# Four moves in the last quarter of a two-layer graph kernel: prefix sum, statistics, a second DMA queue, a view per indirect store

## The chip, the cores and the metric

The kernel runs on one core of one Trainium2 chip. The metric is device time of an execution in microseconds (us), median of several executions. The kernel before takes 683.77 us (median of 3 runs, 682.87 to 683.98). A profile is one such execution; its span is about 1.7 us shorter than the time.

## The reference

Two layers on N = 2708 nodes with D = 512 features, followed each by a layer norm (cut):

```python
def _L0_gnn_ref(x, adj, W, b):
    d_inv_sqrt = jnp.where(rowsum > 0, rowsum ** (-0.5), 0.0)
    support = (d_inv_sqrt[:, None] * adj * d_inv_sqrt[None, :]) @ x
    return jax.nn.relu(support @ W + b)
def _L1_gnn_ref(nodes, adj, W_node, b_node, K, ...):      # attention, 4 heads
    ...
    logits = s[:, :, None] + NEG * (1.0 - adj)[None]      # NEG = -1e10
    attn = jax.nn.softmax(logits, axis=-1)
    ...                                                   # mean over heads, relu
x = _layernorm(x + _L0_gnn_ref(...)); x = _layernorm(x + _L1_gnn_ref(...))
```

The entries of `adj` lie between 0.05 and 1, so NEG * (1 - adj) leaves each row of the second layer a single neighbour, that of its largest entry. The kernel therefore gathers one row of u = relu(h·M + c) per node (M and c fold the weights together) and checks on the chip that this held; a dense path stands ready if not.

## The kernel before

The first layer runs over eleven pairs of row blocks (m = 0 to 10), each in eleven steps of k (at_k = 0 to 10). A step turns four adjacency tiles on TensorE, ScalarE copies them to SBUF, VectorE makes four sums of them, and TensorE multiplies. After a pair, VectorE combines the products, and the rows of the pair before go through h·M. A block is 128 rows (74 in the last pair, blocks 20 and 21). The program's order on each engine is the order of the source.

While the last pair runs, the gathers for blocks 0 to 15 go out, eight ahead of the statistics. Rows whose neighbour lies in the last pair must wait for its u, so they are set aside in a list: a flag marks them, a prefix sum of the flags (two small matmuls) gives each its place, and GpSimd turns the places into one-hot rows, with which TensorE writes the list. These "listed rows" are gathered and written last, by two indirect stores.

The parts that the change touches, and those that the argument needs:

```python
def store(dst, t, ib):
    for lo, hi, r0 in parts(ib):          # two parts for a block of 74 rows
        nc.sync.dma_start(out=dst[r0 + lo : r0 + hi, :], in_=t[lo:hi])
...
out_early, out_late = dram_disjoint_views(out, 2)
...
def ahead(i):                             # transposes and copies for step i
    ...
    nc.scalar.copy(aT[:kr, :4, :pr], ps[:kr, :, :pr])
    nc.vector.tensor_add(s(S1), s(L21), s(L22))   # and three more
...
def store_u(ib, po):
    nc.vector.tensor_add(ut[:pr], po[:pr], c_bc[:pr])
    nc.scalar.activation(ut[:pr], ut[:pr], AF.Relu)
    store(u_late if ib >= NE else u_early, ut, ib)        # NE = 20
...
def fetch_row(ib):                        # an indirect DMA from GpSimd
    gs[ib] = mix.tile([P, D], F32, name="g", bufs=8)
    fetch(gs[ib], pr, idx[:pr, ib : ib + 1], u_d if ib >= NE else u_early)
...
for i, (m, k) in enumerate(steps):
    ...
    if m == NM - 3 and at_k == NM - 1:    # NM = 11
        ps = counts(flag_b)               # prefix sum: two matmuls
    ahead(i + 2)
    ...
    products(i, banks, at_k == 0, at_k == NM - 1)
    ...
    elif final:                           # the last pair
        if at_k == 0:
            home(0); home(1)              # ten loads of 256 KB, own rows
        elif at_k == 2:
            for ib in range(*chunk(0)):   # blocks 0 to 4
                fetch_row(ib)
        elif at_k == 3:
            for ib in range(PER, PER + 3):
                fetch_row(ib)             # blocks 5 to 7
            for n in range(NL):           # NL = 2 blocks of listed rows
                fetch(hs[NB + n], P, to_read[:, n : n + 1], h_d)
        elif 6 <= at_k:
            n = (at_k - 6) * 2
            for ib in (n, n + 1):
                stats(ib, P)              # add, bn_stats, bn_aggr on VectorE
                if n + 8 < 16:
                    fetch_row(ib + 8)
            if at_k == 8:   home(2); home(3); spread(*chunk(0))
            elif at_k == 9: shift_of(*chunk(0)); chunk_out(0)
            elif at_k == 10: spread(*chunk(1))
    if at_k == NM - 1:
        new = combine(m, banks)           # opens with nc.scalar.copy(s1, p1)
...                                       # tail: last two blocks, chunks 1 to 3
for n in range(NL):                       # rows whose neighbour lies in the last pair
    normalize(NB + n, P)
    nc.gpsimd.indirect_dma_start(out=out_early[:, :], ...)
```

`chunk_out(c)` normalizes five blocks on ScalarE and stores each through SyncE's queue.

## Time and profile before

| | kernel before |
|---|---|
| time, median of 3 | 683.77 us |
| the profiled execution | 689.2 us, span 687.4 us |
| TensorE stands for the prefix sum at | 519.8 to 523.0 us, half clock after it |
| TensorE's last product of the last pair ends | 629.21 us |
| first addition of the last combination | 637.35 us |
| second indirect store issued | 682.57 us |

The page's line of busy times gives each engine's busy us, its share of the span and its instructions:

```profile
PE 621.2 (90%) x2810; PEld 460.1 (67%) x2810; DVE 471.6 (69%) x1166; ACT 170.8 (25%) x245; POOL 96.9 (14%) x135
```

TensorE (PE) carries the kernel up to about 630 us, so the averages of the others say little: what matters is who keeps TensorE or the tail waiting, and where. Note the first two rows of the table: the execution that was profiled took 5.4 us more than the timed ones. That turns out to matter.

### The profile page before, as it was taken

To read this page: it belongs to the slowest core of one execution; us is meant where nothing else is said; L and a number is where in the kernel's file an instruction comes from. 1 tells how busy PE (TensorE), PEld (TensorE's weight loads), DVE (VectorE), ACT (ScalarE), POOL (GpSimd) and SP (SyncE) were. 2 spreads that over 40 slices of the span, in tenths; PEclk is the share of its full clock that TensorE was granted. 3 is DMA by queue.
4 is the path that set the end of the run, shared out by engine and by line. 5 is a ranking of instruction groups with operands and counts; after the bars stand their busy time and mean duration, and the time that the engine had idled before them with its cause. 6 is when DMAs were issued, how large, how long until landed. Compare 5 with 4: busy or idle time off the path is not lost. (4 is left out here: it accounts for less than half of the span.)

```text
span 687.4 us, 7915 instructions
## 1 busy us (share of the span) xinstructions
PE 621.2 (90%) x2810; PEld 460.1 (67%) x2810; DVE 471.6 (69%) x1166; ACT 170.8 (25%) x245; POOL 96.9 (14%) x135
## 2 busy tenths in 40 slices
PE   5999979999999999999999999999998999996420
PEld 3545434787878878878788788787886787563100
DVE  2356886998785856957858569578587479329773
ACT  2544455111112121211121212111211111201333
POOL 1011321000000001000000010000002260055442
PEclk9999999999999999999999999999997999998565
DMA  8999899213050141410501414104014010758743
GB/s 340 417 379 403 329 366 301 92 33 161 31 193 31 60 187 39 172 53 31 193 31 59 188 39 173 51 32 192 31 60 97 31 62 0 251 163 272 238 137 118
DMA packets 30774, 103.73 MB, mean 151 GB/s; under 512 B 4169, under 2 KB 4169, under 8 KB 25568
## 3 DMA queue, kind: packets, MB, share of 16 engines
q1 hardware_dynamic: 28008, 96.30, 38.2%
q0 software_dynamic: 2720, 6.86, 3.3%
q8 instruction: 24, 0.39, 0.2%
q14 instruction: 22, 0.18, 0.1%
HBM read 85.64 MB, written 17.77 MB: 150 GB/s over the span
## 5 line engine op out<-in xcount | busy, mean ns | idle before, releaser
L360 PE MATMUL bank<-v,aT 128*128 128x256 f32 (+3 forms) x968 | 270.1, 382 | 0.4 <-DVE t L382 0.4
L360 PE MATMUL bank<-t,aT 128*128 128x256 f32 (+3 forms) x726 | 197.9, 381 | 1.2 <-DVE u L387 0.8
L360 PEld LDWEIGHTS bank<-v,aT 128*128 128x128 f32 (+3 forms) x968 | 171.8, 187 | 23.5 <-DVE t L382 0.6
L360 PEld LDWEIGHTS bank<-t,aT 128*128 128x128 f32 (+3 forms) x726 | 135.7, 187 | 24.0 <-DVE u L387 1.2
L333 ACT COPY aT<-tp 128x512 f32<-128x512 f32 (+3 forms) x121 | 68.5, 568 | 263.6 <-PE tp L331 246.4
L338 DVE TENSOR_TENSOR aT<-aT 128x128 f32<-128x128 f32 (+3 forms) x121 | 33.9, 281 | 88.4 <-ACT aT L333 87.4
L197 PE MATMUL po<-w_sb,sT 128*128 128x512 f32 (+1 forms) x176 | 79.9, 598 | 3.3 <-DVE sT L191 3.3
L197 PE MATMUL po<-m_sb,sT 128*128 128x512 f32 (+1 forms) x176 | 81.1, 615 | 0.0
L331 PE MATMUL tp<-ident,a 128*128 128x128 f32 (+3 forms) x484 | 71.3, 270 | 0.3 <-ACT aT L333 0.3
L421 DVE MAX8 top<-a 128x8 f32<-128x1354 f32 (+1 forms) x44 | 68.8, 1563 | 0.0
L422 DVE FIND_INDEX8 at<-top,a 128x8 uint32<-128x1354 f32 (+1 forms) x44 | 68.7, 1562 | 0.0
L331 PEld LDWEIGHTS tp<-ident,a 128*128 128x128 f32 (+3 forms) x484 | 58.2, 139 | 14.6 <-issue 5.3
L272 ACT ACTIVATE junk<-a 128x2708 bf16<-128x2708 f32 (+1 forms) x22 | 54.1, 2461 | 47.9 <-DMA a<-in_adj_dram 47.9
L408 POOL TENSOR_SCALAR rs<-mv 128x1 f32<-128x1 f32 (+1 forms) x22 | 7.7, 350 | 398.5 <-DVE mv L406 398.5
L197 PEld LDWEIGHTS po<-m_sb,sT 128*128 128x128 f32 (+1 forms) x176 | 33.9, 194 | 40.7 <-issue 40.1
L197 PEld LDWEIGHTS po<-w_sb,sT 128*128 128x128 f32 (+1 forms) x176 | 31.4, 188 | 36.9 <-issue 32.9
L430 DVE TENSOR_TENSOR ut<-po,c_bc 128x512 f32<-128x512 f32 (+1 forms) x22 | 15.1, 690 | 41.2 <-PE po L197 41.2
L270 DVE COPY v<-po 128x512 f32<-128x512 f32 (+1 forms) x22 | 15.2, 690 | 34.3 <-PE po L197 34.3
L431 ACT ACTIVATE ut<-ut 128x512 f32<-128x512 f32 (+1 forms) x22 | 13.8, 630 | 100.2 <-DVE ut L430 96.5
L341 DVE TENSOR_TENSOR aT<-aT 128x128 f32<-128x128 f32 (+3 forms) x121 | 35.1, 290 | 4.2
L340 DVE TENSOR_TENSOR aT<-aT 128x128 f32<-128x128 f32 (+3 forms) x121 | 33.7, 279 | 0.0
L339 DVE TENSOR_TENSOR aT<-aT 128x128 f32<-128x128 f32 (+3 forms) x121 | 33.7, 279 | 0.0
(137 smaller groups left out, 433.3 us busy)
## 6 DMA issues: line engine op xcount, KB each, us to landing
a<-in_adj_dram SPq DMA_DIRECT2D x38, 1354.0 KB
v<-in_x_dram SPq DMA_DIRECT2D x20, 256.0 KB
xr<-in_x_dram SPq DMA_DIRECT2D x20, 256.0 KB
h_d<-t SPq DMA_DIRECT2D x20, 256.0 KB
u_d<-ut SPq DMA_DIRECT2D x20, 256.0 KB
a<-h_d SPq DMA_DIRECT2D x20, 256.0 KB
out_dram<-a SPq DMA_DIRECT2D x20, 256.0 KB
kh<-in_L_gnn_K_dram SPq DMA_DIRECT2D x3, 1024.0 KB
```

Of the source, the lines that this page charges most:

```text
L197: nc.tensor.matmul(po[:pr], sT[:, f, :pr], wt[:, f, :], start=(f == 0), stop=(f == ND - 1))
L270: nc.vector.tensor_copy(v[:pr, ib, :], po[:pr])
L272: nc.scalar.activation(junk[:pr], a[:pr], AF.Copy, accum_out=sums[:pr, ib : ib + 1])
L331: nc.tensor.transpose(ps[:kr, q, :pr], raw[m][q // 2][:pr, lo : lo + kr], ident[:pr, :pr])
L333: nc.scalar.copy(aT[:kr, :4, :pr], ps[:kr, :, :pr])
L338: nc.vector.tensor_add(s(S1), s(L21), s(L22))
L339: nc.vector.tensor_sub(s(S3), s(L11), s(L21))
L340: nc.vector.tensor_sub(s(S2), s(S1), s(L11))
L341: nc.vector.tensor_sub(s(S4), s(L12), s(S2))
L360: nc.tensor.matmul(banks[bank][:pr, side, :], aT[:kr, left, :pr], right, start=first and side == 0, stop=last, skip_group_check=True,)
L421: nc.vector.max(out=top[:pr, ib, hf, :], in_=part)
L422: nc.vector.max_index(out=at[:pr, ib, hf, :], in_max=top[:pr, ib, hf, :], in_values=part)
```

## The change

Four things, each meant to take a wait off the path: the prefix sum's matmuls move behind other work of TensorE (with the ranks and one-hot rows that hang on them); the statistics of the gathered blocks move from steps 6 to 10 of the last pair to steps 5 to 9; u of the last four blocks is stored from ScalarE's DMA queue, not behind the loads in SyncE's; and each indirect store gets its own view of the output, so that the second needn't wait for the first.

```diff
-    def store(dst, t, ib):
+    def store(dst, t, ib, queue=nc.sync):
...
-            nc.sync.dma_start(out=dst[r0 + lo : r0 + hi, :], in_=t[lo:hi])
+            queue.dma_start(out=dst[r0 + lo : r0 + hi, :], in_=t[lo:hi])
-    out_early, out_late = dram_disjoint_views(out, 2)
+    out_views = dram_disjoint_views(out, 1 + NL)
+    out_late = out_views[NL]
...
-        store(u_late if ib >= NE else u_early, ut, ib)
+        store(u_late if ib >= NE else u_early, ut, ib, nc.scalar if ib >= NE - 2 else nc.sync)
...
-            store(out_early, hs[ib], ib)
+            store(out, hs[ib], ib)
...
-        if m == NM - 3 and at_k == NM - 1:
+        if m == NM - 2 and at_k == 0:
             ps = counts(flag_b)
...   (ranks, one-hot rows and listing: one step later each)
-            elif 6 <= at_k:
-                n = (at_k - 6) * 2
-                for ib in (n, n + 1):
+            if 5 <= at_k < 10:
+                for ib in range(at_k * 2 - 10, at_k * 2 - 8):
                     stats(ib, P)
-                    if n + 8 < 16:
+                    if ib + 8 < 16:
                         fetch_row(ib + 8)
...   (spread and shift_of: a step sooner; chunk_out and home stay in steps 9 and 8)
-            out=out_early[:, :],
+            out=out_views[n][:, :],
```

More of the change, by code (lines that the diff above doesn't have):

```diff
@@ L627, in tile_two_graph_layers @@
             hTs[2 * (m - 1) + q] = turn(done[q], rows(2 * m - 2), nc.scalar.copy)
-        if m == NM - 3:
-            if at_k == NM - 2:
-                flag, flag_b = first_indices()
-            elif at_k == NM - 1:
+        if m == NM - 3 and at_k == NM - 2:
+            flag, flag_b = first_indices()
+        if m == NM - 2:
+            if at_k == 0:
                 rank = ranks(flag, ps)
-        elif m == NM - 2:
-            if at_k < 5:
-                for ib in range(at_k * 4, at_k * 4 + 4):
+            if 1 <= at_k < 6:
+                for ib in range(at_k * 4 - 4, at_k * 4):
                     hot(rank, ib)
-            if at_k == 2:
+            if at_k == 3:
                 ls = p_o.tile([P, D], F32, name="po")
-            if 2 <= at_k < 7:
-                for ib in range(at_k * 4 - 8, at_k * 4 - 4):
+            if 3 <= at_k < 8:
+                for ib in range(at_k * 4 - 12, at_k * 4 - 8):
                     enlist(ls, ib)
@@ L666, in tile_two_graph_layers @@
                 nc.vector.tensor_copy(bad_i, po[:1, :1])
-            elif 6 <= at_k:
-                n = (at_k - 6) * 2
-                for ib in (n, n + 1):
+            if 5 <= at_k < 10:
+                for ib in range(at_k * 2 - 10, at_k * 2 - 8):
                     stats(ib, P)
-                    if n + 8 < 16:
+                    if ib + 8 < 16:
                         fetch_row(ib + 8)
-                if at_k == 8:
-                    home(2)
-                    home(3)
-                    spread(*chunk(0))
-                elif at_k == 9:
-                    shift_of(*chunk(0))
-                    chunk_out(0)
-                elif at_k == 10:
-                    spread(*chunk(1))
+            if at_k == 7:
+                spread(*chunk(0))
+            elif at_k == 8:
+                home(2)
+                home(3)
+                shift_of(*chunk(0))
+            elif at_k == 9:
+                chunk_out(0)
+                spread(*chunk(1))
         if at_k == NM - 1:
```

## The prediction

> **What bounds the kernel now.** I read the page first. Its busy rows show TensorE full from about slice 7 to slice 36, and one dent in the row of the granted clock.
>
> ```profile
> span 687.4 us, 7915 instructions
> ...
> PE   5999979999999999999999999999998999996420
> ...
> PEclk9999999999999999999999999999997999998565
> ```
>
> One digit is 17.2 us. The dent (a 7) is at 515 to 533 us; after 629 us TensorE is nearly done and the end belongs to others. So a microsecond counts in two places: where TensorE stops before 629 us, and on the path after it. Next I asked who kept TensorE waiting after 500 us (the waits of PE: the waiter, whom it waited for, total us, times, longest).
>
> ```profile
> PE tp L189 <- DVE t L415: 16.9, 2, 16.3
> PE po L475 <- DVE flag_b L470: 3.3, 1, 3.3
> PE tp L189 <- ACT aT L333: 0.3, 1, 0.3
> ```
>
> The second line is the prefix sum's matmul, the first the gap of the last pair. The timeline of PE there (start, duration):
>
> ```profile
> 519.17 0.59 PE L360 MATMUL bank<-v,aT 128*128 128x256 f32 x2
> 523.02 0.17 PE L475 MATMUL po<-flag_b,before 128*128 128x20 bf16 x1 [3.25 <-DVE flag_b L470]
> ...
> 525.66 1.91 PE L360 MATMUL bank<-t,aT 74*128 74x256 f32 x4
> ...
> 529.93 8.36 PE L197 MATMUL po<-m_sb,sT 128*128 128x512 f32 x16
> 538.13 0.60 PE L331 MATMUL tp<-ident,a 128*128 128x128 f32 x4
> ```
>
> TensorE stands still for 3.25 us, and afterwards four products take 1.91 us where they took 1.03 before. The stage view from 523 to 532 us gives a granted clock of 0.50, and 1.00 on either side. For the last pair I read the timelines of ACT, DVE and POOL:
>
> ```profile
> 610.38 0.41 ACT L333 COPY aT<-tp 128x296 f32<-128x296 f32 x1 [3.14 <-PE bank L360]
> 618.37 0.71 ACT L333 COPY aT<-tp 128x296 f32<-128x296 f32 x2 [7.58 <-PE tp L331]
> ...
> 633.43 3.63 ACT L579 ACTIVATE a<-a,nbs,rss 128x512 f32<-128x512 f32 x5 [12.81 <-DVE nbs L575]
> 636.97 0.35 ACT L381 COPY s<-bank 74x256 f32<-74x256 f32 x1
> ```
>
> ```profile
> 603.87 1.26 POOL L553 DMA_INDIRECT g<-u_d,idx  x1 [17.65 <-DMA u_d<-ut]
> ...
> 678.94 1.05 POOL L744 DMA_INDIRECT out_dram<-listed,to_put  x1 [1.84 <-ACT listed L579]
> 682.57 0.99 POOL L744 DMA_INDIRECT out_dram<-listed,to_put  x1 [2.58 <-issue]
> ```
>
> TensorE's last product ends at 629.2 us, but the copy that opens its combination (L381) starts at 636.97 and the first add (L382) at 637.35: 8 us late. VectorE is still in the statistics (to 636.3) and ScalarE in five normalizations queued ahead of the copy. From there one chain runs to the end: combine, layer norm, turn, times M, u, its store, the gathers from 661.94, statistics, normalization, two indirect stores. The second store waits 2.58 us.
>
> **What the Trainium skill says.** "TensorE: Matmul & The Clock Gate", Part 1, states that an idle window of about 3.4 us halves the clock and that the window is free-running. The trace agrees: 3.25 us idle, then 0.50. "DMA: Bandwidth & Descriptors", section "Issuing engines are not separate DMA queues", says that DMAs from different engines run on the same 16 engines and interleave; its section "Queues, rings and completion order" gives SP and ACT each a ring and lets an engine go round-robin between them. No transfer of this trace was issued by ACT, so it can't show that yet. The section "Anatomy of one DMA" of the same page gives a fixed cost of some 2 us to completion; the second store's wait of 2.58 us agrees.
>
> **The change, part by part.**
>
> 1. Prefix sum a step on. The step view of PE (start to start of its transposes) is 3.46 us for a plain step and 10.33 us for a pair's last step with its two products by M, in each of the seven pairs before. Here the two are 6.93 and 15.06 (523.07 to 538.13): 8.20 us too long, of which 3.3 is the wait and the rest half clock. In the new order the matmul stands behind the eight products by M (about 7 us of work), so flag_b, ready at 522.96, is long there. That removes 8.2 us; two small matmuls cost about 0.15. What it moves: the ranks (13 VectorE operations, 525.84 to 528.0, 2.15 us) leave the path to the combination and go into a step where VectorE idles. The 20 one-hot rows on GpSimd begin later. Before, four were made at 528.24 to 531.9, far ahead; now each group has two steps (7.4 us) less two small operations of the layer norm. Four take 3.7 to 3.9 us against a step of 3.70, and the layer norm's pair of POOL operations (0.9 us) comes in twice. By my count the rows 8 to 11 are ready 0.75 us after TensorE wants them and the rest nearly on time: TensorE loses about 0.8. Net 8.2 - 0.15 - 0.8 = **7.2 us**, all on the path, since the last pair follows TensorE.
>
> 2. Statistics a step sooner. A block costs 0.68 + 0.69 + 0.18 us, 1.53 from start to start; a step of two blocks and the aT adds (0.85) is about 4.0 us against TensorE's 3.28. Started after the adds that end at 611.6 (the gathers landed 3 to 4 us after issue, so blocks 0 and 1 are there), five such rounds, the last without adds, end at about 629.9. The five normalizations run 626.8 to 630.5, the copy follows, the combination starts at about 630.9 instead of 637.35: 6.5 us in this profile. But here the first block began only at 619.53, because the copy ready to start at 613.6 was held until 618.37 by something the trace does not explain (TensorE's transposes had ended). Without that hold the old order would have begun at 614.9 and combined at 633.2: a gain of only 2.3 us. The profiled run took 689.2 us and the timed ones 683.8, so part of this hold may not be there in the timed runs. I chose **3.8 us**, nearer the low end.
>
> 3. u stored from ScalarE's queue. Before, the stores were issued at 596.20 and 598.36 behind ten loads of 256 KB on SP's ring, and the first gather went at 603.87. On its own ring I estimate 2 us sooner. With part 2 the statistics begin at 611.6, after even the old gathers had landed (607.6 and on), so this is hidden. At the end SP's ring is empty when u goes out (654.7 to 659.6); a hop between engines, **0.2 us**. ScalarE pays 0.3 to 0.5 us per issue, where it has room.
>
> 4. A view per indirect store. In the built program the second store no longer waits for the first. POOL's gathers start 1.25 us apart, so it goes at 680.2 instead of 682.57: 2.4 us sooner, less some sharing as both move 256 KB together: **2.2 us**, at the very end.
>
> Sum: 7.2 + 3.8 + 0.2 + 2.2 = 13.4 us; 683.8 - 13.4 = **670.4 us**.
>
> **The rivals.**
>
> - The hold of ScalarE's copy is real, and either goes (then the statistics bring 6.5: 667.7 us) or moves with the gathers, 2 us earlier, onto the copy of the step before. Then the statistics start only at about 616 and the gain falls to 1.5 us: 672.7. For it: the hold ends as the gathers end. Against it: nothing in the dependencies ties them.
> - GpSimd becomes the bound in the one-hot stretch: 20 rows of 0.95 us in five steps of 3.7. If TensorE waits 2 to 3 us there, and especially if the clock halves again, half of part 1 goes back: about 674 to 676 us. Against it: a wait of under 1 us by my count, in pieces.
> - The end is bound by moving bytes, so two indirect stores together land no sooner: 672.6. Against it: 256 KB landed within 2.4 us of the end of issue, most of it fixed.
> - The clock at the last products by M falls differently. In the profile eight logical products took 9.39 us there against 7.03 at full clock; this is worth up to 1.2 us either way.
>
> **Range and chances.** The parts vary from 10.5 us (statistics 1.5, one-hots 1.5 worse) to 16.5 (hold real and gone), hence 667.0 to 674.0 us for 8 in 10. 2% of 683.8 is 13.7 us, so the line is at 670.1, just below my number: faster by over 2% 0.45, within 2% 0.54, slower 0.01. Every part removes a wait that the trace shows on the path or is hidden, so slower is remote.
>
> **What would show it.** Right: no wait of PE for flag_b and no half clock before the last pair; steps of 3.46 and about 10.5 us there; PE's last product at about 622 us; the first add of the combination within 2 us of it; the second indirect store 1.3 us after the first; the first gather within 4 us of the second u store. Wrong: PE waits for a hot row above 1 us in total; ScalarE's copies of the last pair held again, with VectorE idle before the statistics; the second store landing late.

## The result, and the profile after

The changed kernel took 673.55 us (median of 4, 673.23 to 675.08), the kernel before 683.32 us in the same call (median of 4). All were in the fast state. The ratio is 0.9861, 95% interval 0.9843 to 0.988: within 2%. (A ratio is the mean time of one kernel's fast runs over that of the other's in the same rounds, so not quite the ratio of the medians.) That is 9.8 us gained where 13.4 were predicted; the time lies inside the range.

The page of the kernel after, the lines that answer to those shown of before:

```profile
span 671.5 us, 7913 instructions
...
PE   5999988999999999999999999999999999999420
...
PEclk9999998999999999999999999999999999999675
```

The dent in the clock at three quarters of the span is gone. From the waits of TensorE in the kernel after, 500 to 690 us (columns as in the prediction), the one that is new:

```profile
PE po L513 <- POOL hot L508: 0.6, 1, 0.6
```

Its timeline of TensorE where the prefix sum now stands:

```profile
520.33 0.60 PE L332 MATMUL tp<-ident,a 128*128 128x128 f32 x4
523.79 7.03 PE L198 MATMUL po<-m_sb,sT 128*128 128x512 f32 x16
530.65 0.17 PE L476 MATMUL po<-flag_b,before 128*128 128x20 bf16 x1
530.71 0.64 PE L332 MATMUL tp<-ident,a 128*128 128x128 f32 x4
```

The step is 3.46 us and the next 10.38, as in other pairs; the prefix sum follows the products by M without a gap, and those take 7.03 us where they took 8.36 at half clock. The only wait for a one-hot row is 0.6 us. ScalarE's timeline in the last pair of the kernel after:

```profile
610.41 0.41 ACT L334 COPY aT<-tp 128x296 f32<-128x296 f32 x1 [2.88 <-DVE mvs L567]
613.70 0.40 ACT L334 COPY aT<-tp 74x296 f32<-74x296 f32 x1 [2.88 <-PE tp L332]
619.94 3.63 ACT L580 ACTIVATE a<-a,nbs,rss 128x512 f32<-128x512 f32 x5 [5.84 <-DVE nbs L576]
623.48 0.35 ACT L382 COPY s<-bank 74x256 f32<-74x256 f32 x1
```

And GpSimd's timeline, the first gather and the two indirect stores:

```profile
597.69 1.26 POOL L554 DMA_INDIRECT g<-u_d,idx  x1 [17.98 <-issue]
...
665.00 1.05 POOL L743 DMA_INDIRECT out_dram<-listed,to_put  x1 [1.84 <-ACT listed L580]
666.35 0.99 POOL L743 DMA_INDIRECT out_dram<-listed,to_put  x1 [0.30 <-issue]
```

No copy of ScalarE is held here: they come every 3.3 us. The normalizations start at 619.94 and the first addition comes at 623.86, 1.2 us after TensorE's last product. The second indirect store waits 0.30 us instead of 2.58.

To compare traces whose starts differ by a microsecond, I measure the last pair from one mark: the set of four transposes just ahead of the eight products by M of the pair before (574.68 us before, 568.16 after). The expectations below call it the pair's first transposes; it is in fact the second set, but the same in every run. From the mark to the first addition it was 62.67 us before and is 55.70 after. That is 7 us, not the 3.8 that I gave the statistics. With the prefix sum's 7.25 us (from a common point at 516.14 and 516.87 us to the mark, 58.54 and 51.29 us) and 2.4 us of the tail, the two profiles differ by nearly 16 us. The timed runs differ by 9.8. So the profile of before probably shows something that its timed runs had not: the hold of ScalarE's copy. (This is inferred: no trace of the kernel before from a call in which it took 683 us was kept.) Of the 2.4 us of the tail, 1.1 go with the clock of TensorE's last products by M, which took 9.39 us before and 8.27 after; over all fourteen profiles they lie anywhere from 8.23 to 9.73 us.

### The profile page after: what moved, and what is told of

It is laid out like the page before. It is cut to its first block, busy times and chain, and to the rows that moved or that the text cites. A ratio compares the mean times of both kernels' runs of the same rounds, so it can differ in the third digit from the quotient of the medians.

```text
span 671.5 us, 7913 instructions
## 1 busy us (share of the span) xinstructions
PE 616.4 (92%) x2810; PEld 457.8 (68%) x2810; DVE 472.4 (70%) x1166; ACT 171.0 (25%) x245; POOL 98.8 (15%) x135
## 4 chain that ended last, share of the span: by engine, by line
PE 73%; DVE 16%; POOL 4%; DMA 2%; issue 2%; ACT 1%; POOLq 0%; SPq 0%; ACTq 0%; DVEq 0%
PE bank L361 44%; PE po L198 20%; PE tp L332 6%; PE tp L190 3%; DVE at L423 2%; DVE top L422 2%; POOL hot L508 2%; DMA g<-u_d,idx 1%; DVE st L566 1%; DVE km L279 1%; DMA v<-in_x_dram 1%; DVE a L564 1%; PE po L303 1%; DVE v L217 1%; DVE aT L342 1%
## 5 line engine op out<-in xcount | busy, mean ns | idle before, releaser
L198 PE MATMUL po<-m_sb,sT 128*128 128x512 f32 (+1 forms) x176 | 78.6, 600 | 0.0
```

What stands on the lines that cost most here:

```text
L198: nc.tensor.matmul(po[:pr], sT[:, f, :pr], wt[:, f, :], start=(f == 0), stop=(f == ND - 1))
```

## The experiments

All runs were correct and in the fast state. The kernel before ran beside each, but not at the same speed in every call: 683.3 us in the call above, 688.91 in that of the first four runs below, 688.88 and 688.17 in the next two, and 683.44 in the last. I therefore compare ratios, and traces of like calls.

Distances from the mark, in us, from each run's trace. The copies of the last pair usually start 3.3 us apart; one that starts over 4 us after the one before it is called held:

| run | parts of the change | TensorE's last product | first addition | held copies |
|---|---|---|---|---|
| before, first profile | none | 54.53 | 62.67 | yes |
| before_again | none | 54.54 | 62.42 | yes |
| prefix_only | prefix | 54.53 | 62.29 | yes |
| stats_only | statistics | 58.71 | 61.85 | yes |
| views_only | views | 55.29 | 62.00 | yes |
| queue_only | queue | 54.53 | 61.67 | yes |
| after, first profile | all | 54.53 | 55.70 | no |
| after_again | all | 60.62 | 62.26 | yes |
| no_stats | all but statistics | 56.09 | 62.65 | yes |
| no_queue | all but queue | 56.53 | 61.51 | yes |
| early_queue | queue only half | 57.98 | 61.98 | yes |
| copies_dve | no queue, copies moved | 59.95 | 62.29 | yes |
| thin_gathers | no queue, fewer gathers ahead | 54.53 | 55.47 | no |
| thin_late_stats | the same, statistics late | 54.53 | 59.02 | no |

### before_again: is the hold a matter of one profile?

The kernel before, unchanged.

> The kernel before, unchanged, profiled a second time. Theory 1: the hold of ScalarE's aT copy (610.8 to 618.4 us in the first profile) was an event of that one profiled run; then no copy of the last pair waits over 3.3 us, the first add of the last combination comes about 4 us sooner after the pair's start than the 52.5 us of the first profile (so about 48), and the span is about 682. Theory 2: the hold belongs to the order of the program; then it is there again, over 6 us, with a span near 687. Timed: a ratio of 1.000 within 0.2% in either case.

It took 689.03 us, ratio 1.000 (0.9991 to 1.0009). In its trace the same copy is held: it should follow the one at 611.30 by 3.3 us and starts at 619.02. In this call the timed runs, too, take 689. So the hold is no accident of one profile; the theory that it was fell. It belongs to a call (that is, perhaps, to a chip), and the first profile of before was of that kind while its timed runs were not.

### prefix_only, stats_only, views_only, queue_only: each part alone

Each applies the hunks of one part of the diff above to the kernel before, and nothing else:

```diff
 # prefix_only
-        if m == NM - 3 and at_k == NM - 1:
+        if m == NM - 2 and at_k == 0:
             ps = counts(flag_b)
...   (ranks, one-hot rows and listing a step later)
 # stats_only
-            elif 6 <= at_k:
+            if 5 <= at_k < 10:
...
 # views_only
-            out=out_early[:, :],
+            out=out_views[n][:, :],
 # queue_only
-        store(u_late if ib >= NE else u_early, ut, ib)
+        store(u_late if ib >= NE else u_early, ut, ib, nc.scalar if ib >= NE - 2 else nc.sync)
```

> Only the prefix sum a step on. From the profile: the wait for flag_b and the half clock before the last pair are gone (8.2 us), one-hot rows cost about 0.8, so 7.3 us faster, about 676.0, ratio 0.9893. Rival: part of it is given back in the last pair, because TensorE runs ahead of the gathers and statistics; then 4 to 6 us.

> Only the statistics a step sooner. Theory 1 (no hold in a usual run): the combination starts at most 2.3 us sooner, so 0 to 2.3 us, ratio 0.9966 to 1.000. Theory 2 (hold in every run, cured by the new order): 5 to 6.5 us, ratio 0.990 to 0.993. If the gathers were the bound (first gather at 603.9): the statistics wait for them and the gain is near 0.

> Only the view per indirect store. The second store goes 1.3 us after the first instead of 3.6: 2.2 us faster, ratio 0.9968. Rival: both stores share the DMA engines and land no sooner: 0 to 0.8 us.

> Only u stored from ScalarE's queue. Hidden: ratio 1.000 within 0.1%, hold in the trace as before. Rival: it cures the hold, 3 to 5 us faster where before takes 689.

| run | time, us | before in the same call | ratio (95%) |
|---|---|---|---|
| prefix_only | 680.97 | 688.91 | 0.9884 (0.9866 to 0.9902) |
| stats_only | 688.75 | 688.91 | 0.9993 (0.9983 to 1.0002) |
| views_only | 687.31 | 688.91 | 0.9977 (0.9963 to 0.999) |
| queue_only | 690.64 | 688.88 | 1.0021 (1.0012 to 1.0031) |

The prefix sum brings 8.0 us, the views 1.6. The statistics bring nothing that the interval shows, and the queue costs 1.5 us. ScalarE's timeline in stats_only tells why the first of these failed:

```profile
618.76 0.41 ACT L333 COPY aT<-tp 128x296 f32<-128x296 f32 x1 [6.37 <-PE tp L331]
625.90 0.70 ACT L333 COPY aT<-tp 128x296 f32<-128x296 f32 x2 [6.73 <-remote]
634.21 3.63 ACT L579 ACTIVATE a<-a,nbs,rss 128x512 f32<-128x512 f32 x5 [7.61 <-DVE nbs L575]
```

Now two copies are held, by about 3.5 and 3.8 us, instead of one by 4.4. The statistics stand behind those copies in VectorE's order, so they start 7 us sooner (613.1 us against 620.2 in before_again), but the normalizations that close them start at 634.21 against 634.08. TensorE's last product, which waits for the second held copy, slips from 630.1 to 635.0. All that was won at the start of the statistics is lost inside them. That the new order moved the hold isn't shown, though: views_only, with the old order, also has two held copies (by 2.0 and 2.5 us), so the place of the hold differs between single profiles. In GpSimd's timeline of views_only the second indirect store waits as little as in the changed kernel:

```profile
678.44 1.05 POOL L745 DMA_INDIRECT out_dram<-listed,to_put  x1 [1.84 <-ACT listed L580]
679.80 0.99 POOL L745 DMA_INDIRECT out_dram<-listed,to_put  x1 [0.30 <-issue]
```

### after_again, no_stats, no_queue: the change whole, and less one part

```diff
 # no_stats, against the changed kernel
-            if 5 <= at_k < 10:
+            elif 6 <= at_k:
...
 # no_queue, against the changed kernel
-        store(u_late if ib >= NE else u_early, ut, ib, nc.scalar if ib >= NE - 2 else nc.sync)
+        store(u_late if ib >= NE else u_early, ut, ib)
```

> The changed kernel, unchanged, a second time. Four profiles of the old order of the gathers show ScalarE's copy of the last pair held for 4 to 5 us while gathers run; the one profile of the changed kernel does not, but it came from another call, in which the kernel before took 683.3 and not 688.9 us. If the hold belongs to the call (its chip), then in a call where before takes about 689 this kernel shows it too and the ratio stays near 0.986. If the change cures it, then such a call gives about 673.5, ratio 0.977.

> The changed kernel with the statistics a step later, as before (parts 1, 3 and 4). If the statistics are worth nothing, as in their run alone (0.9993), this is as fast as the changed kernel: 0.1% either way. If they are worth the 3.8 us of the prediction once TensorE runs ahead: 0.55% slower than the changed kernel.

> The changed kernel with u stored from SP's queue (parts 1, 2 and 4). The first gather came 29.5 us after the start of the last pair's first transposes with ScalarE's queue and 28.9 to 29.2 with SP's, so no earlier: the same time as the changed kernel within 0.1%. Rival: the hold of ScalarE's copy comes with SP's queue and goes with ScalarE's; then 2 to 5 us slower, with the hold in the trace.

Beside a kernel before of 688.88 us, after_again took 680.0 (ratio 0.9862, 0.9829 to 0.9894), no_stats 680.25 (0.9869, 0.9837 to 0.99), and no_queue 678.52 (0.9844, 0.9813 to 0.9875). So the change wins about 9 us here as well, but from a start 5.5 us higher, and its trace now has the hold. The same kernel with and without the hold can be set side by side: its first addition comes at 62.26 and 55.70 us from the mark, 6.6 us apart, and its timed runs, 680.0 and 673.55 us, are 6.5 us apart. Leaving out the statistics costs 0.25 us: again they bring nothing that the intervals show. Leaving out the queue gains 1.5 us by the medians, as much as it cost alone; the ratios' intervals overlap, but the four runs of no_queue (678.06 to 678.77) all lie below the four of after_again (678.79 to 680.5). By its median no_queue is better than both kernels of the case in this call.

ScalarE's timeline in after_again:

```profile
602.57 0.41 ACT L334 COPY aT<-tp 128x296 f32<-128x296 f32 x1 [3.15 <-PE tp L332]
610.48 0.41 ACT L334 COPY aT<-tp 128x296 f32<-128x296 f32 x1 [7.50 <-PE tp L332]
616.95 0.71 ACT L334 COPY aT<-tp 128x296 f32<-128x296 f32 x2 [6.06 <-PE tp L332]
```

TensorE's timeline in the same run:

```profile
613.98 0.23 PE L332 MATMUL tp<-ident,a 74*74 74x74 f32 x1 [1.72 <-issue]
615.38 0.22 PE L332 MATMUL tp<-ident,a 74*74 74x74 f32 x1 [1.17 <-issue]
```

The copy that should start at 605.9 starts at 610.48, and TensorE lets single transposes through, 1.2 to 1.7 us apart, with no wait that the profile can name. The transposes that ScalarE's held copy names as releaser had ended at 605.8. GpSimd's gathers, meanwhile, go out every 1.25 us. A rival would be that the engines wait for their own instructions, which have DMA queues of their own in the profile. The DMA view speaks against it, though no run tests it: from 602 to 617 us it lists the gathers' queue alone, and the next packet of an instruction queue comes at 617.5 to 618, after the second held copy had started (616.95).

The queue's cost shows in the tail. ScalarE's timeline there in after_again (ACTq is the issue of DMAs from ScalarE):

```profile
646.66 1.30 ACTq L101 DMA_DIRECT2D u_d<-ut  x2
649.89 0.63 ACT L432 ACTIVATE ut<-ut 74x512 f32<-74x512 f32 x1 [3.25 <-DVE ut L431]
650.54 1.02 ACTq L101 DMA_DIRECT2D u_d<-ut  x2
651.61 3.63 ACT L580 ACTIVATE a<-a,nbs,rss 128x512 f32<-128x512 f32 x5 [1.09 <-DVE a L564]
```

And in no_queue:

```profile
649.48 0.63 ACT L432 ACTIVATE ut<-ut 74x512 f32<-74x512 f32 x1 [3.25 <-DVE ut L431]
650.38 3.63 ACT L580 ACTIVATE a<-a,nbs,rss 128x512 f32<-128x512 f32 x5 [0.27 <-DVE nbs L576]
```

Two stores of 1.02 us together stand before the five normalizations, which start 1.09 us after ScalarE's last work rather than 0.27. Their stores to the output then start later (652.45 us against 651.25), and the last gathers are late too: from the issue of the first of these (653.89 and 653.49 us) to VectorE's first use of it it takes 9.1 us with the queue and 7.7 without. And the queue brought the first gather no sooner: it is issued 29.5 us after the mark in the changed kernel, 29.2 before, 29.0 in queue_only and 28.9 in prefix_only. In the kernel before, the first u store did stand 1.3 us behind the loads (u ready at 594.90 us, store at 596.20), but the second, for which the gathers wait too, did not (598.33 and 598.36): it is issued 23.68 us after the mark before and 23.63 after. From there to the first gather it took 5.5 us before and 5.9 after.

### early_queue: is the queue's cost all in the tail?

```diff
-        store(u_late if ib >= NE else u_early, ut, ib)
+        store(u_late if ib >= NE else u_early, ut, ib, nc.scalar if NE - 2 <= ib < NE else nc.sync)
```

> The change without its new queue, plus that queue for the u of the next to last pair alone (blocks 18 and 19), not for the last two blocks in the tail. Theory A (the queue costs only in the tail: there ScalarE issues four stores of 0.5 to 0.65 us each between the two activations and the normalizations of the third chunk, so that chunk's stores start 1.2 us later and run into the last gathers): the cost goes, the ratio to the kernel before is that of the version without the queue, 0.984, and the third chunk's first normalization comes no more than 0.4 us after its shift. Theory B (the landing of u through the second queue costs too): about 0.986, and the first gather comes later than 28.9 us after the last pair's first transposes.

It took 679.41 us beside 688.17 (ratio 0.9867, 0.9842 to 0.9891). The third chunk's first normalization comes at most 0.27 us after its shift, as theory A has it, and from the last activation of u to the second indirect store it is 22.0 us (23.8 in after_again, 22.3 in no_queue), so the tail's cost is gone in the profile. But the ratio is not that of no_queue; the first gather was issued 29.7 us after the mark, and the intervals overlap. This is inconclusive: part of the queue's cost may lie before the tail.

### copies_dve: is it ScalarE that is held?

Without the queue, and with the copies of steps 6 to 10 of the last pair on VectorE:

```diff
-        nc.scalar.copy(aT[:kr, :4, :pr], ps[:kr, :, :pr])
+        if m == NM - 1 and k >= 6:
+            nc.vector.tensor_copy(aT[:kr, :4, :pr], ps[:kr, :, :pr])
+        else:
+            nc.scalar.copy(aT[:kr, :4, :pr], ps[:kr, :, :pr])
```

> The change without its new queue, with the copies of the transposed tiles for the last pair's steps 6 to 10 on VectorE. Theory S1 (ScalarE alone is held, and VectorE and TensorE wait behind it): the hold goes, the statistics of ten blocks take 18 to 20 us as in the profile of the changed kernel without the hold, rather than 24.5, and the ratio is about 0.977 to 0.979. Theory S2 (what holds ScalarE holds whatever engine copies there, or TensorE's transposes are late themselves): the copies on VectorE are late by as much, statistics again in 24 us, ratio 0.984 or above.

679.72 us beside 688.17, ratio 0.9869 (0.9843 to 0.9894). VectorE's timeline has the copies late in the same places:

```profile
610.43 0.47 DVE L335 COPY aT<-tp 128x296 f32<-128x296 f32 x1 [2.41 <-PE tp L332]
...
617.57 0.47 DVE L335 COPY aT<-tp 128x296 f32<-128x296 f32 x1 [2.76 <-remote]
```

Their starts are 6.8 and 7.1 us after the copy before, where 3.3 is usual. Theory S1 falls: whatever holds ScalarE's copy holds VectorE's too. The releaser named is again a set of transposes that had ended at 606.9 us.

### thin_gathers: do the gathers bring on the hold?

Without the queue. Four buffers for gathered blocks 0 to 15, so that a gather waits for the statistics of the fourth block before it; four others for blocks 16 to 19; and the two gathers of listed rows in the pair's last step:

```diff
-        gs[ib] = mix.tile([P, D], F32, name="g", bufs=8)
+        late = 16 <= ib < NE
+        gs[ib] = mix.tile([P, D], F32, name="g2" if late else "g", bufs=4)
...
-                for ib in range(*chunk(0)):
+                for ib in range(4):
                     fetch_row(ib)
...
-                for ib in range(PER, PER + 3):
-                    fetch_row(ib)
-                for n in range(NL): ...            # listed rows
...
-                    if ib + 8 < 16:
-                        fetch_row(ib + 8)
+                    fetch_row(ib + 4)
...
+            elif at_k == 10:
+                for n in range(NL): ...            # listed rows
...   (in the tail, blocks 14 and 15 beside 18 and 19)
```

> The change without its new queue, with four gathers ahead rather than eight in the last pair and the two gathers of listed rows moved to its last step, so the ten back to back gathers become four. Theory H1 (the unexplained hold of ScalarE's copies in the last pair is brought on by the dense run of gathers): no copy from the eighth on waits over 4 us, TensorE's last product ends some 4 us sooner after the pair's start (52 rather than 56.5 us), and the ratio goes from 0.984 to about 0.977. Theory H2 (the hold goes with the chip or the place in the program, not with the gathers): the copies are held as long as before, 4 to 8 us, ratio 0.983 to 0.987. If this call's chip shows no hold in the kernel before (it then takes 683 us rather than 689), both give the same.

672.68 us (672.32 to 673.4) beside 688.17: ratio 0.977, 0.9749 to 0.9791. No copy is held. ScalarE's timeline in thin_gathers, the copies and the combination's first copy:

```profile
606.23 0.41 ACT L334 COPY aT<-tp 128x296 f32<-128x296 f32 x1 [2.86 <-PE tp L332]
609.51 0.41 ACT L334 COPY aT<-tp 128x296 f32<-128x296 f32 x1 [2.87 <-DVE mvs L568]
...
622.34 0.35 ACT L382 COPY s<-bank 74x256 f32<-74x256 f32 x1
```

GpSimd's timeline there, the fourth gather and the fifth, which waits 3.74 us for the statistics:

```profile
600.38 0.95 POOL L554 DMA_INDIRECT g<-u_d,idx  x1 [0.30 <-issue]
605.07 0.95 POOL L554 DMA_INDIRECT g<-u_d,idx  x1 [3.74 <-DVE a L565]
```

Theory H1 stands, with the ratio that it gave: in the same call early_queue (679.41 us) and copies_dve (679.72) have the hold, and here it is gone. Where H1 erred is TensorE's last product, which it had at 52 us from the mark: it is at 54.53, as in every trace in which TensorE isn't kept waiting. The hold doesn't look like a limit of bytes. In the stage view (bounds in us, then length, busy time and count of TensorE, weight loads, VectorE, ScalarE, GpSimd, granted clock, DMA share, GB/s), after_again has:

```profile
610.00:620.00 10.00, 6.30 (x23) 3.74 (x22) 6.21 (x18) 1.11 (x3) 4.50 (x5) 0.84 0.62 188
```

and thin_gathers:

```profile
610.00:620.00 10.00, 10.00 (x51) 6.78 (x50) 9.55 (x27) 1.60 (x3) 6.46 (x7) 1.00 0.83 267
```

Without the hold more is moved in the same stretch, 267 GB/s against 188, and TensorE is never idle. What was taken away is the run of gathers issued back to back: in after_again fourteen follow one another with pauses of 0.3 to 0.6 us, here four. The run alone doesn't make a hold: the first profile of the changed kernel has it too, and no held copy. Two edits were made together, so whether the depth or the place of the listed rows' gathers did it isn't parted.

On this chip this version is faster than both kernels of the case: the changed kernel took 680.0 us there, in a call whose kernel before took 688.88 us, and this one 672.68, beside 688.17. Some 1.5 us of that are the queue. It was not timed on a chip of the quick kind.

### thin_late_stats: what are the earlier statistics worth without the hold?

The version above with the statistics back at steps 6 to 10:

```diff
-            if 5 <= at_k < 10:
-                for ib in range(at_k * 2 - 10, at_k * 2 - 8):
+            if 6 <= at_k:
+                for ib in range(at_k * 2 - 12, at_k * 2 - 10):
...   (spread, shift_of and chunk_out as in the kernel before)
```

> The version with four gathers ahead, which runs without the hold (ratio 0.977), with the statistics of the gathered blocks put back to steps 6 to 10, as in the kernel before: what the earlier statistics are worth where nothing holds ScalarE's copies. Theory E1 (they are worth the 2.3 us that the prediction had for a last pair without the hold, up to the 3.8 us that it chose, and the hold ate that in the other runs): about 675 to 676.5 us where the kernel before takes 688, ratio 0.9805 to 0.9825, and the first addition of the last combination comes 2.3 to 3.8 us later after the pair's first transposes than the 55.5 us with the earlier statistics. Theory E2 (they are worth nothing whatever the gathers do): ratio 0.976 to 0.978 and that distance within 0.7 us of 55.5.

This call was of the quick kind: the kernel before took 683.44 us, so the ratio (0.9895, 0.9877 to 0.9913) isn't comparable with that expected. The time, 676.62 us, is just above the 675 to 676.5 that theory E1 gave for a call of the other kind, and the distance from the mark to the first addition is 59.02 us against 55.47, 3.55 us later, inside E1's 2.3 to 3.8. E2 falls. VectorE's timeline shows one line that belongs to the thinning and not to the statistics:

```profile
623.74 0.69 DVE L565 TENSOR_TENSOR a<-a,g 128x512 f32<-128x512 f32 x1 [1.57 <-DMA g<-u_d,idx]
```

Here the late statistics catch up with their gathers and wait 1.57 us for one. Without that wait VectorE would be ready for the addition at about 625.6 us, but ScalarE's copy that it needs starts only at 625.74, so the addition would come at about 626.1 instead of 627.20. That leaves an estimate of 2.5 us as the statistics' own worth, near the 2.3 that the prediction worked out for a pair without the hold. It rests on one profile each from two chips; the two versions were not run in one call.

## Why the prediction was right or wrong

The time (673.55 in a range of 667.0 to 674.0) and the class (within 2%, the likelier by a little) came out as predicted, the time partly by luck. It lies 0.45 us inside the range. The gain, 9.8 us, lies outside the 10.5 to 16.5 us from which the range was made: 683.8 - 10.5 is 673.3, the range was set out to 674.0, and the kernel before ran at 683.32 us in this call. Nor do the ends follow from the terms named for them: 13.4 less 2.3 (statistics at 1.5) and 1.5 (one-hot rows) is 9.6, and with the hold gone it is 16.1. The sum, 13.4 us, was 3.6 us too high. Its terms:

1. **Prefix sum, 7.2 us.** Right. The profiles give 7.25 us up to the mark, and the part alone brings 8.0 us of time. The wait and the half clock are gone, the one-hot rows cost 0.6 us by the view of waits, where 0.8 was worked out. One reading was too generous: 3.25 us of standing doesn't fill the idle window of about 3.4 us that the prediction cites, and half clock had begun after only 2.6 of them (519.76 to about 522.4).
2. **Statistics, 3.8 us.** This is the term that was mis-sized. The prediction had 2.3 us for a pair without the hold and 6.5 for one where the hold vanishes, and chose between. No run showed the second case: on chips that have the hold, it stays, on other copies, and eats the gain (0.25 and 0.5 us measured, neither clear of noise), which the first rival had named, with 1.5 us; without the hold the estimate above is 2.5 us. (Two small sums of this part are off: five rounds of 4.0 us from 611.6, the last without 0.85, end at 630.8, not 629.9; and a start at 614.9 instead of 619.53 brings 637.35 to 632.7, not 633.2.) The 7 us between the two first profiles is a comparison of an execution with the hold to one without. The sign was on the page: 689.2 us profiled beside 683.8 timed. The prediction used it to lean towards the lower number, but not all the way.
3. **Queue, +0.2 us.** Wrong in sign: about -1.5 us. The step that failed is that the first gather waits for the loads in SyncE's ring. The last u store, which sets it, was issued as soon as u was ready in both kernels, and the sign that the prediction named, the first gather within 4 us of it, did not come (5.9 us). "ScalarE pays ... where it has room" failed too, in the tail, where it hasn't.
4. **Views, 2.2 us.** Right in mechanism, smaller in size: 1.6 us (interval of the ratio: 0.7 to 2.6 us).

With 8.0, -1.5 and 1.6 in place of these terms, the 9.8 us measured in the first call leave 1.7 for the statistics. This is arithmetic across calls, not a measurement of its own. Of the rivals, a GpSimd bound in the one-hot stretch and an end bound by bytes did not come about; the hold stayed, on other copies, on two of the chips, though the gathers went no sooner than before; the clock of the last products by M did fall differently (9.39 and 8.27 us in the two profiles), and no run parts it from the rest.

What stays open: what ties a dense run of gathers to the copies and transposes of other engines, and why only in some calls. The two kinds came on different chips (the quick call whose chip is known was on another chip than the slow ones; the chip of the first call isn't on record), but three chips are too few to say that it is the chip. Nor is it known whether the queue costs something ahead of the tail.

## What to carry to other kernels

When the profiled execution is slower than the timed ones by more than the usual scatter, find what the profile has that the timed runs lack before any of its waits is counted as a gain. A wait that no dependency explains is best tested by taking away what runs beside it, not by moving work around it: moving the statistics or the copies brought nothing that the intervals show, fewer gathers issued ahead brought 5 us by the ratios. And here a DMA issued from an engine that computes cost that engine's time in its order (1.02 us for two stores ahead of the normalizations), so it belongs where that engine has room.

## What the Trainium skill lacked or had wrong

- No page has that beside a run of ten or more indirect gathers from GpSimd, 1.25 us apart, copies on ScalarE or VectorE and single transposes on TensorE can be held that wait for nothing the profile shows. The traces from calls where the kernel before took 688 to 689 us show holds of 1.3 to 5.0 us each, and none with four gathers ahead (672.68 us, against 679.41 and 679.72 with the hold in the same call).
- "TensorE: Matmul & The Clock Gate", Part 1, has the full clock return after one busy window of about 3.4 us or more. In the profile before, TensorE stood 3.25 us and was then busy throughout, yet half clock lasted 10.2 us (522.4 to 532.6), three such windows; near 102.6 us of the same trace it lasted one. The page doesn't say when it takes more than one. And half clock had begun after 2.6 us of standing, less than the idle window of about 3.4 us that the page has for it.
- "DMA: Bandwidth & Descriptors", section "Issuing engines are not separate DMA queues", calls the sequencer's time for issuing usually small beside the DMA, but not what it costs an engine with work of its own. In the tail it was 1.30 and 1.02 us of ScalarE for two stores each, the latter just ahead of five normalizations, and the whole move cost about 1.5 us.
